# Second sublayers' soft MoE tokens: transposed by VectorE in 32-squares and placed through DRAM instead of by TensorE

## The chip, the cores and the metric

The kernel runs on one core of a Trainium2 chip. A core has five engines with a queue each: TensorE (PE; its weight loads are shown apart as PEld), VectorE (DVE), ScalarE (ACT), GpSimd (POOL) and SyncE (SP), which here issues every DMA. Engines wait for one another through semaphores, and each queue is in order. The metric is device time in microseconds (us), the median of several runs; one further execution was recorded by the hardware profiler.

## The reference

Input `x` has 8 batches of 256 tokens of 128 channels, all in float32. Six residual sublayers follow one another; the change is in the third, which computes the same as the first, with the same weights:

```python
x = x + 0.5 * _L0_ffn_ref(_layernorm(x), ...)   # soft MoE, "first sublayer"
x = x + _L0_attn_ref(_layernorm(x), ...)        # linear attention
x = x + 0.5 * _L0_ffn_ref(_layernorm(x), ...)   # soft MoE, "second sublayer": changed
x = x + 0.5 * _L1_ffn_ref(_layernorm(x), ...)   # gated MLP with two hidden layers
x = x + _L1_attn_ref(_layernorm(x), ...)        # FAVOR+ attention
x = x + 0.5 * _L1_ffn_ref(_layernorm(x), ...)
```

The soft MoE, with E = 16 experts of S = 64 slots:

```python
x = _layernorm(x, norm_g, norm_b)
se = _layernorm(slot_embeds, slot_g, slot_b) * scale
logits = einsum('bnd,esd->bnes', x, se)
dispatch = softmax(logits, axis=1)                   # over the tokens
combine = softmax(logits.reshape(b, n, -1), axis=-1) # over all slots
slots = einsum('bnd,bnes->besd', x, dispatch)
gate = gelu(einsum('besd,edf->besf', slots, Wg) + bg)
up = einsum('besd,edf->besf', slots, Wu) + bu
eout = einsum('besf,efo->beso', gate * up, Wd) + bd
out = einsum('bns,bso->bno', combine, eout)
```

## The kernel before

**Stages.** The eight batches form two groups of four. For each group `group(g)` goes through the sublayers: MoE (`layer` 0), linear attention, MoE again (`layer` 1), gated MLP (`glu`), FAVOR+ attention (`favor`), gated MLP. The two groups are interleaved, so that matmuls of one cover the dependent chains of the other.

**The MoE of one batch.** `dispatch` normalizes the 2 x 128 tokens of a batch (TT = 2 tiles `y` of 128 tokens by 128 channels): VectorE's statistics, GpSimd's inverse root (`root`), and two applications on GpSimd or VectorE. `transposed` then makes `yt`, channels by tokens, since a matmul contracts over the partitions: two TensorE transposes ("flips", L452, a matmul with the identity) into PSUM, and one `affinely` step that reads PSUM, multiplies by `norm_g`, adds `norm_b` and writes `yt` in SBUF, on ScalarE (L557) or VectorE (L559). `replicated` sends `y` through DRAM into another layout for a later matmul. Four logits steps (L670, four matmul instructions each) read `yt`. The softmax over the tokens follows (maximum on VectorE, exponentials on ScalarE, L709, division on GpSimd, 32-square transposes on VectorE), then `gather` (L749) forms the slots. `experts` fetches each expert's weights `we` (L864), runs the hidden matmuls (L878) and the down matmuls (L909), and `back.place` (L922) puts results into the slots by DMA. `combine` (L952) brings them back to tokens and adds them to `x`. In `linear`, L1000 is the last projection, whose sum `x` is what the second MoE's normalization reads.

**Transposing without TensorE.** `linear`, `glu` and `favor` already transpose their tokens in another way, `squares_turned`: VectorE transposes every 32x32 square in place (L513), one DMA spills the tile to DRAM (L516), and four DMAs place the squares into a tile of channels by tokens (L522, each 32 partitions). Both are steps on SyncE, and the placement waits for the spill's landing.

**The order.** The program first lists its steps (2490), each with its reads, its writes and an estimated cost. `ORDER` is a list of step numbers written out: a step runs on the first engine that it allows, or, where the number is negative (-1 - n), on the second. `Plan.place` goes through the list, gives each step a start by the estimates, and gives tiles their buffers from pools of fixed size (`kinds`; `k1` has 14 of 256 floats a partition, `ps` is the eight PSUM banks); `issue` emits the steps by these starts. So `ORDER` settles each engine's queue and which engine takes a movable step. Where the plan expects TensorE to wait over 700 ns for a step, `idle` (L1503) issues matmuls of the identity that compute nothing, besides 14 of them at the head.

Of the kernel before, what the change touches and what calls it, by code (L numbers as in the profile page):

```python
# [10 lines left out]
AF = mybir.ActivationFunctionType  # L11
ALU = mybir.AluOpType
AX = mybir.AxisListType
P = 128

ORDER = (
    10, 0, 3, 2, 1, 37, 38, 6, 7, 5, 9, 8, 19, 20, 12, 13, 11, 40, 39, 41, 22, 31, -22, 23, 24,
    42, 43, 62, 63, 130, 14, 16, 131, 25, 15, 17, 18, 4, 132, 133, 134, 26, 135, 44, -29, -28, 60,
    32, -34, 83, -35, 61, 138, 139, 84, -87, 1347, 161, 29, 30, 68, 1268, 140, 141, 54, 35, -86,
    89, 90, -37, 1297, 162, 69, 146, 70, 64, 65, 66, 67, -164, 73, 142, 143, 144, 145, 87, 88, 93,  # L20
    95, 114, 71, 91, -165, 167, 165, 1269, -1272, 74, 75, 76, 94, 97, 96, 166, 175, 151, 92, 98,
    147, 136, 72, 1348, -1350, -1351, 152, 173, 77, 99, 100, 192, 104, 174, 78, 82, 176, 81,
    -1271, 1272, 1273, 105, 169, 1298, -1300, -1301, 1301, 80, 101, 79, 102, 115, 106, 137, 170,
    1274, 153, 1303, 1302, 168, 103, 1353, 182, 1354, 107, 108, 154, 1276, 171, 1278, 172, 53, 45,
    1281, 1275, 1282, 1277, 1280, 1279, 1305, 1306, 148, 183, 177, 1284, 1285, 178, 1283, 1307,
    184, 155, 109, 1304, 111, 47, 112, 113, 149, 150, 156, 179, 185, 186, 180, 46, 110, 1286,
    1309, 1308, 157, 181, 187, 193, -190, 1310, 1312, 330, 1313, 320, 158, 159, 160, 190, 1292,
    191, 188, 331, 351, 334, 335, 1315, 1314, 1311, 324, 325, 194, 1331, 1332, 332, 321, 322,
    1333, 355, 362, 333, 257, 366, 215, 367, 352, 336, 57, 353, 368, 195, 354, 356, 357, 363, 364,
    348, 349, 369, 196, 1293, 219, 216, 217, 1334, 326, 341, 323, 370, 365, 246, 197, 198, 199,  # L30
    371, 1287, 1316, 372, 373, 220, 221, 299, 1351, 1352, 1317, 337, 261, 116, 262, 218, 117, 258,
    259, 345, 346, 342, 361, 338, 204, 260, 263, 232, 288, 200, 347, 247, 343, 344, 1357, 1358,
    248, 1355, 249, 350, 250, 251, 1376, 1288, 374, 233, 1377, -1379, 1294, 252, -1380, 118, 274,
    275, 1335, 358, 359, 303, 264, -1357, 1366, 1321, 304, 305, 300, 202, 277, 265, 289, 301, 302,
    1295, 292, 208, 319, 309, 290, 1336, 212, 1322, 209, 316, 119, 1363, 1318, 1359, 317, 291,
    206, 293, 1296, 1289, 1380, -1382, 236, 237, 240, 1319, 294, 1323, 210, 1290, 211, 213, 214,
    1360, 1382, 235, 313, 314, 55, 1320, 278, 306, 307, 310, 315, 120, 311, 1337, 222, 282, 318,
    312, 279, 241, 242, 1364, 327, -1362, 1291, 283, 284, 225, 229, 280, 281, 1324, 121, 230, 124,
    122, 328, 1325, 267, 226, 256, 238, 239, 234, 271, 231, 227, 228, 268, 269, 298, 1362, 272,
    1365, 339, 308, 207, 340, 253, 295, 270, 360, 254, 243, 273, 244, 203, 123, 285, 296, 125,  # L40
    286, 1371, 1372, 223, 201, 1373, 1374, 1375, 276, 1367, 266, 1326, 1327, 205, 255, -1329,
    1389, 1390, 1392, 1393, 375, 126, 127, 1384, -1331, 1368, 1400, 50, 128, 1338, 1385, 1386,
    -1388, 1395, 56, 1401, 1402, 1369, 1370, 287, 1396, 224, 129, 1397, 329, 245, 297, 377, 454,
    1388, 1391, 1403, 1329, 1404, 1398, 1399, 376, 378, 455, 402, 456, 457, 458, -460, -461, 464,
    1383, 461, 462, 379, 380, 1394, 1405, 1408, 1409, -1407, 1517, 403, 404, 428, 429, 1407, 463,
    1475, 1518, 1519, 465, 1343, 430, 405, 1521, 1411, 467, 466, -471, -382, 471, 1522, 1520,
    1523, -383, 383, 1479, 1480, 1476, 1477, 1478, 406, 1534, 1535, 1485, 1486, 1489, 1490, 1580,
    1410, 1412, 1581, -408, -409, 409, 1582, 1481, 431, 1491, 1487, 1496, 1497, 1500, 1501, 432,
    1583, -434, 1498, 468, 412, 1499, 1506, 384, 1502, 1507, 1488, 1492, 1493, 1510, 1511, 1413,
    410, 52, 1584, 1513, 1514, 1569, 1345, 1585, 1508, 1509, 1570, 1571, 1573, 1414, 1572, 411,  # L50
    414, 1537, 1464, 1503, -435, 435, 385, 1512, 1468, 469, 1465, 1504, 388, 1466, 1467, 1586,
    387, 1574, 1575, 1469, 1470, 413, 418, 1590, 436, 415, 1415, 1591, 472, 1433, -393, 1437,
    1341, 393, 1346, 1426, 1430, 51, 437, 389, 1587, 473, 440, 445, 416, 417, 1588, 1482, 419,
    390, 391, 1559, 1416, 394, 395, 1431, 1432, 1427, 396, 397, 1560, 1592, 474, 475, 398, 399,
    1483, 386, 1428, 1429, 1524, 1525, 439, 441, 1505, 1417, 1420, 1434, 1438, 1440, 1441, 1435,
    400, 1561, 1562, 1424, 1527, 1528, 420, 1454, 1436, 442, 1531, 1484, 401, 1439, 1529, 480,
    481, 421, 443, 48, 438, 483, 1548, 49, -445, 1593, 1526, 1532, 1533, 1563, 476, 477, 1515,
    1530, 1458, 1459, 1460, 482, 478, 479, 1549, 1550, 446, 447, 1552, 484, 588, 422, 589, -486,
    1553, -592, -591, 1494, 1551, 1564, 1589, 1545, 1546, 448, 449, 1443, 1565, 1455, 1456, 1342,
    1442, 1536, 490, 423, 1538, 1554, 450, -452, 1457, -492, 496, 497, 424, 425, 488, -490, 492,  # L60
    594, 1453, 1344, 452, 1339, 1340, 1450, 1451, 499, 1418, 426, 427, 453, 500, 1452, 1447, 592,
    559, 560, -562, -563, 509, 510, 1542, 501, 493, 593, 1576, 1577, 1578, -495, 1543, 504, 1539,
    1540, 596, 597, 495, 1566, 1567, 1544, 1444, 1445, 1541, 58, 598, 498, 599, 512, 604, 1547,
    1446, -512, 1448, 1579, 600, 1449, 563, 1568, -565, 601, 1419, 603, 502, 1422, 505, 513, 514,
    1555, 1471, 1472, 1473, 1556, 1425, 1474, 607, 1461, 1462, 506, 569, 1516, 1557, 567, 605,
    570, -603, 612, 568, 571, 1558, 575, 576, 1463, 572, 574, 503, 608, 609, 573, 486, 522, 523,
    1495, 606, 565, 583, 578, 507, 517, 613, 525, 515, 614, 516, 1421, 610, 543, 1621, 611, 526,
    533, 615, 616, 1620, 579, 580, 1622, 1623, 519, 520, 581, 1423, 518, 521, 1624, -1627, -1626,
    584, 566, 1647, 1646, 1648, 585, 582, 528, 1672, 1673, 534, 586, 535, 536, 1627, 587, 577,
    1594, 529, 1595, 524, 508, 527, 530, 531, 1674, 1596, 1597, 1598, 595, -1601, 617, 619, 487,  # L70
    620, 532, 1628, 1629, 537, 538, 542, -1600, 1601, 1602, 1604, 541, 1632, -619, 1675, 1676,
    -1679, -1678, 1649, 781, 1603, 1606, 621, 1679, 1680, 1650, 1651, 1610, 1605, 544, 545, -540,
    1631, -541, 666, 1652, 1656, 1653, 546, 1607, 1633, 1608, 1609, 1634, 782, 783, 1635, 785,
    -1637, 786, 787, 1611, 1612, 623, 670, 1613, 1637, 792, 796, 793, 805, 797, 798, 547, 1654,
    1630, 622, 708, 709, 710, 712, 713, 548, 624, 714, 1614, 1615, 1681, 711, 667, 668, 784, 655,
    656, 794, 1684, 659, 795, 1683, 799, 1616, 669, 1688, 1655, 1689, 1685, 686, 671, 672, 549,
    657, 658, 660, 625, 1658, 800, 661, -1663, 802, 803, 1657, 1686, 683, 1638, 1682, 1639, 1617,
    1618, 638, 1687, 550, 1619, 639, 553, 554, 725, 1659, 1660, 760, 761, 557, 726, 642, 643, 626,
    627, 684, 673, 1661, 1698, 644, 771, 1663, 1664, 739, 640, 764, 765, 1640, 1641, 645, 641,
    555, 1699, -1702, 772, 773, 674, 1665, 1690, 1691, 743, 740, 1692, 766, 762, -1701, 763, 1666,  # L80
    649, 741, 742, 1642, 1643, 1693, 1702, 1694, -1704, 804, 775, 628, 551, 744, 745, 1706, 1667,
    776, 777, 1644, 1645, 1732, 1695, 1696, 1668, 1669, 687, 629, 1708, 774, 1714, 1733, -1736,
    1697, 1816, 1817, 685, -1819, 646, -1735, 788, 789, 1738, 1819, 778, 779, 780, 675, 647, 1670,
    1671, 1707, 1704, 1710, 648, 665, 1709, 688, 689, 729, 650, 634, 1820, -1822, 632, 651, 1711,
    1712, 690, 1736, 1782, 1783, -1786, 1737, 1717, 691, 1713, 1824, 1716, -1826, 662, 663, 652,
    653, 1715, 1829, 636, 1722, 692, 693, 556, 1718, 790, 1740, 1832, 1833, 1826, 1827, 1830,
    1828, 1719, 1835, 1741, 718, -1785, 1745, 801, 1748, 1749, 1766, 1840, 635, 630, 697, 1786,
    1742, -1744, 1836, 704, 705, 1831, 1834, 1744, 1747, 1750, 654, 1767, 676, 1837, 757, 758,
# [1499 lines left out]
```

## Time and profile before

| What | Value |
|---|---|
| median of 3 runs | 716.48 us (716.41 to 716.98) |
| the profiled execution | 715.34 us |
| its span, first to last instruction | 713.6 us |
| granted TensorE clock | 1.00 |
| flips (L452) | 80: 8 for the keys, 32 in `dispatch`, 16 in `linear`, 24 in `favor` |
| flip duration, min/median/max | 272/273/333 ns |
| stand-in matmuls (L1503) | 66, from 1.6 to 45.2 us |
| 128x256 square transpose (L513), min/median | 414/446 ns |
| spill issue (L516), min/median; placement issue (L522), min/median | 325/328 ns; 557/613 ns |
| one placement, issue to landing, min/median/max | 2.1/2.8/5.3 us |
| DMA packets | 122453, of which 76048 under 512 B |

The profiled execution's time stands 1.7 us over its span, and 1.14 us under the median of the runs. Matmuls are pipelined: a flip's duration overlaps its neighbours', so what one costs TensorE is read from the start of one instruction to the start of the next. A row of the timeline gives the start, the length, the engine, the line, the operation, the tile written and those read, and, in brackets, how long the engine was idle before it and for whom. L452, L557 and the like are line numbers of the kernel before.

### The profile page before, as it was taken

To read this page: it belongs to the slowest core of one execution; us is meant where nothing else is said; L and a number is where in the kernel's file an instruction comes from. 1 tells how busy PE (TensorE), PEld (TensorE's weight loads), DVE (VectorE), ACT (ScalarE), POOL (GpSimd) and SP (SyncE) were. 2 spreads that over 40 slices of the span, in tenths; PEclk is the share of its full clock that TensorE was granted. 3 is DMA by queue.
4 is the path that set the end of the run, shared out by engine and by line. 5 is a ranking of instruction groups with operands and counts; after the bars stand their busy time and mean duration, and the time that the engine had idled before them with its cause. 6 is when DMAs were issued, how large, how long until landed. Compare 5 with 4: busy or idle time off the path is not lost.

```text
span 713.6 us, 14278 instructions
## 1 busy us (share of the span) xinstructions
PE 705.1 (99%) x5218; PEld 606.1 (85%) x5218; DVE 492.5 (69%) x1075; ACT 398.1 (56%) x775; POOL 331.9 (47%) x443
## 2 busy tenths in 40 slices
PE   8999999999999999999999999999999999999998
PEld 6889899998999998998889799786787878869787
DVE  6998867668998779983625444895777777865342
ACT  4978975364892638974536563365243653443421
POOL 6750947345665357465765103535444253342210
PEclk9999999999999999999999999999999999999999
DMA  4464752567263646557354121233213142151000
GB/s 131 135 194 150 210 143 56 184 183 201 65 162 90 175 128 171 126 127 232 110 184 108 45 60 23 45 82 78 65 38 75 26 113 47 38 120 44 8 1 30
DMA packets 122453, 75.00 MB, mean 105 GB/s; under 512 B 76048, under 2 KB 110224, under 8 KB 122384
## 3 DMA queue, kind: packets, MB, share of 16 engines
q1 hardware_dynamic: 122384, 74.09, 39.1%
q8 instruction: 41, 0.67, 0.4%
q14 instruction: 28, 0.23, 0.1%
HBM read 54.06 MB, written 11.62 MB: 92 GB/s over the span
## 4 chain that ended last, share of the span: by engine, by line
PE 89%; ACT 3%; DVE 3%; DMA 2%; POOL 1%; issue 1%; SPq 1%; DVEq 0%; ACTq 0%; POOLq 0%
PE ps L1167 27%; PE ps L878 14%; PE ps L952 8%; PE ps L909 7%; PE ps L749 7%; PE ps L670 5%; PE ps L1265 4%; PE ps L1237 4%; PE ps L1240 4%; ACT comb L709 2%; DMA we<-in_We 1%; PE ps L1342 1%; PE ps L1392 1%; PE ps L452 1%; PE ps L1427 1%; PE ps L1000 1%
## 5 line engine op out<-in xcount | busy, mean ns | idle before, releaser
L878 PE MATMUL ps<-slots,we 128*128 128x256 f32 x512 | 121.1, 380 | 0.8 <-DVE k L915 0.4
L878 PEld LDWEIGHTS ps<-slots,we 128*128 128x128 f32 x512 | 93.4, 190 | 13.3 <-issue 1.0
L1167 PE MATMUL ps<-comb,slots 128*128 128x256 f32 x448 | 103.4, 381 | 0.0
L1167 PE MATMUL ps<-comb,comb 128*128 128x256 f32 x448 | 103.1, 379 | 0.0
L1167 PEld LDWEIGHTS ps<-comb,slots 128*128 128x128 f32 x448 | 83.2, 190 | 13.4 <-issue 2.8
L1167 PEld LDWEIGHTS ps<-comb,comb 128*128 128x128 f32 x448 | 83.8, 190 | 12.6 <-issue 1.7
L884 ACT ACTIVATE k<-ps,small 128x256 f32<-128x256 f32 x128 | 55.8, 475 | 61.5 <-PE ps L878 52.8
L837 POOL TENSOR_TENSOR comb<-comb,k 128x1024 f32<-128x1024 f32 x32 | 75.2, 2362 | 19.1 <-DMA k<-m 8.8
L889 DVE SCALAR_TENSOR_TENSOR k<-ps,small,k 128x256 f32<-128x256 f32 x128 | 57.2, 475 | 31.2 <-ACT k L884 30.4
L722 POOL TENSOR_TENSOR comb<-comb,sm 128x1024 f32<-128x1024 f32 x32 | 60.3, 1897 | 35.7 <-DVE sm L717 28.5
L1181 DVE TENSOR_TENSOR comb<-ps,k 128x512 f32<-128x512 f32 x48 | 32.7, 686 | 56.2 <-PE ps L1167 36.7
L909 PEld LDWEIGHTS ps<-we,k 128*128 128x128 f32 x512 | 64.1, 192 | 2.9 <-issue 0.7
L709 ACT ACTIVATE comb<-comb,sm 128x256 f32<-128x256 f32 x128 | 63.5, 506 | 3.1 <-DVE sm L701 2.5
L909 PE MATMUL ps<-we,k 128*128 128x128 f32 x512 | 64.9, 275 | 0.0
L670 PE MATMUL ps<-k,seT 128*128 128x256 f32 x256 | 61.0, 382 | 1.1 <-ACT k L557 0.9
L457 ACT COPY k<-ps 128x512 f32<-128x512 f32 (+2 forms) x45 | 23.0, 517 | 67.7 <-PE ps L1167 49.2
L952 PEld LDWEIGHTS ps<-slots,comb 128*128 128x128 f32 x512 | 58.7, 192 | 1.5 <-issue 0.7
L952 PE MATMUL ps<-slots,comb 128*128 128x129 f32 x512 | 59.4, 276 | 0.1
L749 PE MATMUL ps<-comb,k 32*128 32x256 f32 x1024 | 58.9, 378 | 0.0
L749 PEld LDWEIGHTS ps<-comb,k 32*128 32x128 f32 x1024 | 53.2, 185 | 3.6 <-ACT slots L557 0.4
L670 PEld LDWEIGHTS ps<-k,seT 128*128 128x128 f32 x256 | 46.8, 190 | 8.6 <-ACT k L557 2.2
L1189 ACT ACTIVATE comb<-comb 128x512 f32<-128x512 f32 x48 | 29.2, 627 | 38.7 <-DVE comb L1181 38.5
(148 smaller groups left out, 1246.3 us busy)
## 6 DMA issues: line engine op xcount, KB each, us to landing
we<-in_We SPq DMA_DIRECT2D x64, 448.0 KB, 4.1
k<-y SPq DMA_DIRECT2D x64, 128.0 KB, 2.9
slots<-k SPq DMA_DIRECT2D x128, 64.0 KB, 2.4
t<-comb SPq DMA_DIRECT2D x8, 512.0 KB, 2.9
k<-t SPq DMA_DIRECT2D x32, 128.0 KB, 3.2
y<-k SPq DMA_DIRECT2D x16, 128.0 KB, 2.5
k<-m SPq DMA_DIRECT2D x8, 256.0 KB, 4.0
t<-k SPq DMA_DIRECT2D x16, 128.0 KB, 1.7
```

The lines of the kernel that those rows point to most:

```text
L670: mm(pl.ap[:, j, :], seT[:, 2 * u + j].rearrange("p k s -> p (k s)"), yt.ap, start=True, stop=True,)
L709: nc.scalar.activation(ex.ap[:, 4 * h + j, :], comb.ap[:, 4 * h + j, :], AF.Exp, bias=mx.ap[:, j : j + 1], accum_out=mx.ap[:, 4 + j : 5 + j],)
L722: return nc.gpsimd.tensor_tensor(ex.ap[:, part], ex.ap[:, part], mx.ap[:, 8:12].unsqueeze(2).to_broadcast([P, 4, N]), ALU.mult,)
L749: mm(po.ap[:, k], yr.ap[rows, TT * (c % 4) + c // 4, :], ex.ap[rows, :, 32 * c : 32 * c + 32], start=(c == 0), stop=(c == N // 32 - 1), ti ...
L837: return nc.gpsimd.tensor_tensor(raw, raw, mb.ap[:, k].unsqueeze(1).to_broadcast([P, 4, N]), ALU.subtract)
L878: mm(pe.ap[:, m, :], we.ap[:, ts(2 * m + c, P)], sl.ap[:, j, k, :, 0:S], start=True, stop=True,)
L884: nc.scalar.activation(ga.ap, pe.ap[:, 0, :], AF.Gelu, bias=bg[:, e, c : c + 1])
L889: nc.vector.scalar_tensor_tensor(ht.ap[:, c, :], pe.ap[:, 1, :], bu[:, e, c : c + 1], ga.ap, ALU.add, ALU.mult,)
L909: mm(po.ap[:, r, :], ht.ap[:, c, ts(r, P)], we.ap[:, ts(4 + c, P)], start=(c == 0), stop=(c == 1),)
L952: mm(po.ap[:, t, 0 : D + 1], comb.ap[:, j, ts(t, P)], eo()[:, j, q, 0 : D + 1], start=(j == 0), stop=(j == NJ - 1),)
L1167: mm(bank.ap[:, o], w(k)[:, c, ts(o, P)], rhs().rearrange("p (c n) -> p c n", c=2)[:, c, :], start=(start and o + c == 0), stop=(stop and ...
L1181: nc.vector.tensor_tensor(C(i, k)(), bank.ap.rearrange("p o n -> p (o n)"), other(), ALU.add)
```

## The change

The `dispatch` of the second sublayer (`plan.tag[1] == 1`, eight batches) takes the way of `squares_turned`. VectorE transposes the squares from `y` into `yt`, out of place, since `replicated` still reads `y`; `yt` is spilled, and the placements write back into the same `yt`; the affine step then runs in place in SBUF. `port=True` tells the plan that, on VectorE, that step keeps GpSimd's next step behind it. A second sublayer's batch has two steps more than before, 2506 in all; `ORDER` is another list throughout, and `k1` has 16 buffers. The first sublayers' `dispatch` keeps the flips.

```diff
 ORDER = (
-    10, 0, 3, 2, 1, 37, 38, 6, 7, 5, 9, 8, 19, 20, 12, 13, 11, 40, 39, 41, 22, 31, -22, 23, 24,
...
+    11, 10, 1, 13, 0, 14, 37, 2, 38, 12, 5, 25, 26, 3, 19, 40, 39, 41, 15, 42, 16, 17, 18, 60, 7,
...
-        "k1": (256, 14),
+        "k1": (256, 16),
...
-    def squares_turned(z, n, cells, dst, out):
+    def squares_turned(z, n, cells, dst, out, src=None):
...
-        step({"DVE": 58 + 1.07 * n}, lambda _: nc.vector.transpose(z(), z()), cells, cells)
+        if src:
+            step({"DVE": 58 + 1.07 * n}, lambda _: nc.vector.transpose(z(), src[0]()), src[1], cells)
+        else:
+            step({"DVE": 58 + 1.07 * n}, lambda _: nc.vector.transpose(z(), z()), cells, cells)
...
     def transposed(y, n, affine=False, squares=False):
         yt = Buf("k1" if n == TT else "k2", (P, n * P))
+        if squares and affine:
+            squares_turned(
+                lambda: yt.ap, n * P, [yt], lambda: yt.ap, [yt],
+                (lambda: y.ap[:, 0:n].rearrange("p t d -> p (t d)"), [(y, t) for t in range(n)]),
+            )
+            affinely(lambda: yt.ap, lambda: yt.ap, [yt], [yt], n * P, True)
+            return yt
...
-    def affinely(dst, src, r, w, n):
+    def affinely(dst, src, r, w, n, port=False):
         def run(e):
             if e == "ACT":
-                nc.scalar.activation(dst(), src(), AF.Identity, bias=nb, scale=ng)
-            else:
-                nc.vector.tensor_scalar(dst(), src(), ng, nb, ALU.mult, ALU.add)
-
-        step({"ACT": act(n, True) + 87, "DVE": dve(n, 120)}, run, [*r, "ng"], w)
+                return nc.scalar.activation(dst(), src(), AF.Identity, bias=nb, scale=ng)
+            return nc.vector.tensor_scalar(dst(), src(), ng, nb, ALU.mult, ALU.add)
+
+        step({"ACT": act(n, True) + 87, "DVE": dve(n, 120)}, run, [*r, "ng"], w, port=port)
...
-        yt = transposed(y, TT, True)
+        yt = transposed(y, TT, True, plan.tag[1] == 1)
```

By the two lists, TensorE's queue before the first expert matmul holds 24 logits steps, six flip pairs of `dispatch` and four gathers in the old order, and 26, seven and four in the new. Steps that may run on two engines are split differently: of the evacuations of PSUM 114 run on ScalarE and 38 on VectorE in the old list, 104 and 48 in the new; of the applications of the normalization 74 on GpSimd and 30 on VectorE, then 63 and 41.

## The prediction

> **What bounds the kernel.** I read the page's busy shares and its chain of waits first, then the stretches of the span, then TensorE's instructions in order of time.
>
> ```profile
> PE 705.1 (99%) x5218; PEld 606.1 (85%) x5218; DVE 492.5 (69%) x1075; ACT 398.1 (56%) x775; POOL 331.9 (47%) x443
> ...
> PE 89%; ACT 3%; DVE 3%; DMA 2%; POOL 1%; issue 1%; SPq 1%; DVEq 0%; ACTq 0%; POOLq 0%
> ```
>
> TensorE (PE) is busy for 705.1 of 713.6 us, and 89% of the chain that ends last is PE. The stretches say the same piece by piece; the columns are the stretch, its length, and busy time with instruction counts for PE, PEld, DVE, ACT and POOL:
>
> ```profile
> 10.00:50.00 40.00, 39.13 (x348) 32.48 (x350) 38.90 (x59) 34.91 (x103) 29.26 (x45) 1.00 0.48 135
> ...
> 150.00:192.00 42.00, 41.76 (x269) 38.23 (x269) 34.95 (x98) 27.36 (x49) 17.62 (x31) 1.00 0.61 161
> ...
> 240.00:285.00 45.00, 44.62 (x285) 41.04 (x284) 36.48 (x94) 27.98 (x64) 26.98 (x32) 1.00 0.53 147
> ...
> 330.00:460.00 130.00, 130.00 (x743) 110.34 (x743) 62.96 (x162) 62.83 (x91) 57.65 (x76) 1.00 0.35 96
> ```
>
> The granted clock is 1.00 throughout. So the time is what TensorE executes plus the few places where it waits. Those places lie early: between 10 and 50 us it runs stand-in matmuls (L1503) that compute nothing, put where the plan expects it to wait.
>
> ```profile
> 14.83 0.61 PE L1503 MATMUL ps<-ident 128*128 128x128 f32 x4
> 15.46 0.76 PE L452 MATMUL ps<-ident,k 128*128 128x128 f32 x2
> ...
> 19.77 0.83 PE L1503 MATMUL ps<-ident 128*128 128x128 f32 x6
> 20.86 2.86 PE L670 MATMUL ps<-k,seT 128*128 128x256 f32 x12 [0.26 <-ACT k L557]
> ...
> 32.40 1.16 PE L1503 MATMUL ps<-ident 128*128 128x128 f32 x8
> 33.78 6.67 PE L670 MATMUL ps<-k,seT 128*128 128x256 f32 x28 [0.23 <-ACT k L557]
> ...
> 44.31 1.16 PE L1503 MATMUL ps<-ident 128*128 128x128 f32 x8
> 45.39 7.19 PE L749 MATMUL ps<-comb,k 32*128 32x256 f32 x128
> ```
>
> From each stand-in to the next real matmul: 0.63, 1.09, 1.38 and 1.08 us, and 0.76 for one more at 26.42; 4.94 us in all.
>
> **Removed from TensorE: 16 flips.** The second-layer `dispatch` runs for eight batches, with TT = 2 flips each. The price of one comes from start to start:
>
> ```profile
> 244.36 1.05 PE L909 MATMUL ps<-we,k 128*128 128x128 f32 x8
> 245.25 0.38 PE L452 MATMUL ps<-ident,k 128*128 128x128 f32 x2
> 245.47 0.61 PE L1029 MATMUL ps<-WqkvT,k 128*128 128x128 f32 x4
> ```
>
> Two flips push the next matmul back by 245.47 - 245.25 = 0.22 us, so 8 x 0.22 = 1.76 us leave the bound engine. This is the safest term: in the two stretches that hold them, 150 to 192 and 240 to 285, TensorE is idle for only 0.24 and 0.38 us. If something else filled the place, the gain would be 0; that is a rival below. The Trainium skill, "TensorE: Matmul & The Clock Gate", Part 4 (PE-mode transpose), gives about 275 ns for one transpose in a kernel; the trace has 272/273/333 ns for these as durations but 0.11 us from start to start, so an estimate by the page (16 x 0.275 = 4.4 us) would count the overlap with their neighbours as gain, and I do not use it.
>
> **Added off TensorE.** Per batch: one 128x256 square transpose on VectorE, one spill to DRAM, four placements of 32 KB, and the affine step as before but reading SBUF. The same parts exist today in `linear` and `favor`: the transpose takes 0.446 us (median), so VectorE gets 8 x 0.446 = 3.6 us against 492.5 busy of 713.6. SyncE issues take 0.33 for the spill and about 0.61 for each placement, 0.33 + 4 x 0.61 = 2.8 us a batch, 22 us in all. From 150 to 190 SyncE's own issues already sum to about 25 of 40 us, so four batches (11 us) fit, but not loosely. The affine step keeps its count. All this costs nothing as long as the tokens land before their logits stand at the head of TensorE's queue.
>
> **The cover.** Old way, flip to affine to logits: about 1 us. New way, by rows: in the first five undisturbed cases of today's squares the time from transpose start to the last landing was 6.8 to 8.2 us, for example here (SyncE, start and length; the transpose began at 124.39, the last piece landed at 132.40):
>
> ```profile
> 124.86 0.34 SPq L516 DMA_DIRECT2D t<-k  x1
> 125.24 0.43 SPq L864 DMA_DIRECT2D we<-in_We  x1
> 126.66 2.61 SPq L522 DMA_DIRECT2D k<-t  x4
> ```
>
> Before it come the batch's last projection (0.61), its add (0.41), the statistics on VectorE (0.94), GpSimd's root (0.19 + 0.19 + 0.70) and two applies (0.90); after it the affine step (0.55). That is 4.5 us around the transfer, 11.3 to 12.7 in all. The new order leaves this much TensorE work between a batch's last projection and its first logits, counted step by step from the listed order and priced by start-to-start rows (0.864 us for a logits or hidden step, 0.45 for a down step): 14.7, 12.8, 17.9 and 18.5 us for batches 0 to 3, and 14.9, 12.0, 22.3 and 11.3 for 4 to 7. So batch 7 could be late by up to 12.7 - 11.3 = 1.4 us and batch 5 by 0.7; at the short end nobody is. I take 0.3 us, from the short end, since the 32 placements that the kernel has today made TensorE wait only once, for 0.5 us (L1298). Bounds: 0 to 2.1. [...]
>
> **What waits behind the wait.** SyncE's queue is in order. In the new order one to four other steps stand between each spill and its own placement: expert weights (L864), token copies (L638) and, for batches 0, 1, 2 and 6, an expert's `back.place` (L922), which waits for VectorE. The spill itself waits for the transpose, and weight fetches stand behind it. Today SyncE waits 109.1 us in total at L516 for such transposes and TensorE waits 0.2 us for weights, so this cover is large.
>
> **The order.** Modes of TensorE's array change 50 times in the old list and 49 times in the new: no term. Before the first expert matmul the old list has 24 logits steps and 6 flip pairs, the new one 26 and 7. That is 2 x 0.864 + 0.22 = 1.95 us of work moved ahead of a point that falls at 54.3 us and is reached with 4.94 us of stand-ins. If the point stays, 1.95 us is gained. Against it: ScalarE also gets one softmax half, a key step, an affine step and an evacuation more before that point, 1.97 + 0.56 + 0.57 + 0.59 = 3.7 us, and from 25 to 43 it runs without a gap. It does wait 2.51 and 1.57 us for the gathers at 46 to 53, so 4.08 us could take it. The gain has bounds of +4.94 (all stand-ins vanish) and -3.7 (ScalarE pushes the point back by all of it); I take half of 1.95, 1.0 us. VectorE's and GpSimd's changes elsewhere have no price of their own: a gain is bounded by TensorE's idle time between 50 and 660 us, 1.5 by the stretches, a loss by the slower rival below, and I take 0. The two more `k1` tiles cost SBUF alone.
>
> **Sum.** -1.76 + 0.3 - 1.0 = -2.46. The profiled execution took 715.34 us (span 713.6 and 1.7 around it), which becomes 712.9. The median of the runs is 1.14 above the profiled one; so 716.48 - 2.46 = 714.0.
>
> **Rivals.**
> - *Flips only.* The head of the kernel stays where ScalarE puts it: 716.48 - 1.76 + 0.3 = 715.0. For it: ScalarE's gapless stretch. Against it: its 4.08 us of waiting at the end of that stretch.
> - *No gain.* The flips' 1.76 us turn into short waits of the same size, as the tokens now come from a chain several times as long: 716.5. For it: SyncE's many issues from 150 to 190. Against it: today's single 0.5 us wait.
> - *Slower: a placement is caught in SyncE's queue.* At 137.33 and 227.48 us a transpose began whose placement landed 14.0 and 11.5 us later, since other steps stood between. If the longer happens to batch 5, 14.0 + 4.5 - 12.0 = 6.5 us of stall fall on TensorE: 716.48 - 1.76 + 6.5 = 721.2. It decides from a stall of 1.76 + 1.43 = 3.2 us (0.2% is 1.43). For it: `back.place` between spill and placement. Against it: batch 6, with the most between, has 22.3 us of cover.
>
> **How the numbers follow.** A measurement of this kernel can tell about 0.2% from no change: faster is below 715.05, slower above 717.91. The forecast has 0.52, flips only 0.20, no gain 0.14, caught placement 0.14. The forecast's own range is 712.3 to 715.2. Faster: 0.50 of the forecast and 0.12 of flips only, 0.62; same: 0.02 + 0.08 + 0.14 = 0.24; slower 0.14. The range goes down to 711.4 (a further 2.6 us, when most of the stand-ins go) and up to 717.0, which takes in no gain and a small stall and leaves out nearly all of the caught placement.
>
> **What would show it.** TensorE's `ps<-ident,k` group falls from 80 to 64; the logits (L670, some lines further down) wait for `k<-t` or the affine step for under half a microsecond in total; stand-ins before the first expert matmul shrink below 4.94 us with that matmul still near 54.3. I am wrong if TensorE's idle time at the logits grows past 2 us, if the first expert matmul comes later than 55.3, or if weights (`we<-in_We`) start to hold TensorE.

## The result, and the profile after

| | before | after |
|---|---|---|
| median of seven runs | 716.48 us (715.90 to 717.54) | 719.04 us (717.64 to 720.03) |
| the profiled execution, its span | 715.34, 713.6 us | 719.04, 717.3 us |

The ratio is 1.0032, with a 95% interval of 1.0021 to 1.0044: the change makes the kernel slower by a third of a per cent. The forecast was 714.0 with a range of 711.4 to 717.0, so both the sign and the range missed.

The page's busy times and its chain of waits, after:

```profile
PE 705.7 (98%) x5200; PEld 605.5 (84%) x5200; DVE 499.3 (70%) x1093; ACT 407.2 (57%) x780; POOL 330.0 (46%) x435
...
PE 53%; DMA 3%; DVE 2%; ACT 1%; SPq 1%; issue 1%; POOL 0%; DVEq 0%; POOLq 0%
```

TensorE issues 18 matmuls fewer (16 flips and two stand-ins), and yet the span is 3.7 us longer. The 53% of the chain can't be held against the 89% before: the profile follows the chain after only back to 281.73 us, and its shares sum to 61%. The stretches of the kernel after (stretch, length, busy time and count for PE, PEld, DVE, ACT and POOL, granted clock, DMA share, GB/s) say where TensorE now stands still:

```profile
10.00:50.00 40.00, 38.02 (x328) 32.12 (x328) 37.79 (x60) 35.27 (x105) 28.34 (x43) 1.00 0.47 133
115.00:150.00 35.00, 34.06 (x319) 31.38 (x318) 23.46 (x67) 16.51 (x29) 19.02 (x27) 1.00 0.46 140
150.00:192.00 42.00, 41.69 (x260) 37.73 (x259) 33.64 (x97) 29.39 (x51) 17.91 (x25) 1.00 0.65 174
240.00:285.00 45.00, 44.68 (x281) 41.05 (x280) 38.82 (x106) 28.29 (x61) 24.45 (x31) 1.00 0.56 154
285.00:335.00 50.00, 47.89 (x483) 43.28 (x482) 36.56 (x78) 32.88 (x85) 28.32 (x25) 1.00 0.55 160
```

Two of the same stretches in the kernel before, which the prediction didn't show:

```profile
115.00:150.00 35.00, 35.00 (x324) 32.73 (x323) 21.90 (x61) 15.03 (x28) 19.38 (x29) 1.00 0.44 129
...
285.00:335.00 50.00, 49.93 (x494) 45.77 (x493) 37.06 (x80) 35.81 (x82) 28.91 (x26) 1.00 0.59 155
```

By busy time, the stretches that hold the changed work, 150 to 192 and 240 to 285, are as full as before. Most of what is lost lies from 115 to 150, before any second-sublayer placement is issued (the first is at 170.9 us), and from 285 to 335: 0.94 and 2.04 us of idle time more. TensorE's waits in the kernel after (line and cause: us in total, times, longest) name the missing things:

```profile
PE ps L888 <- DMA we<-in_We: 1.7, 3, 0.9
PE ps L1513 <- POOL ident masks.py:199: 1.6, 1, 1.6
PE ps L962 <- DMA slots<-k: 1.2, 1, 1.2
PE ps L680 <- ACT seT L603: 1.1, 2, 0.7
PE ps L680 <- ACT k L568: 0.9, 3, 0.4
PE ps L759 <- issue: 0.5, 1, 0.5
PE ps L759 <- DMA k<-y: 0.5, 1, 0.5
```

Before, one such row was for a transfer among these three:

```profile
PE ps L878 <- DMA we<-in_We: 0.2, 1, 0.2
```

Three transfers now hold TensorE for 3.4 us, where before it was 0.2: expert weights (`we`, L888), slot copies by `back.place` (`slots<-k`, the combine at L962) and token copies by `replicated` (`k<-y`, the gather at L759). None of the three is what the change touches. The placed tokens hold it hardly at all: of the 0.9 us at the logits (L680) for the affine step (L568), only 0.2 lies after 55 us.

For a finer sum every kind of matmul is priced by its pitch, its regular distance from start to start (0.216 us for a 128x256 one, 0.112 for a 128x128 one, 0.054 for one of a gather), and the rest of TensorE's time, from its first matmul on, is called unused; it takes in the stand-ins, short waits and slow pitches. The pitched time falls by 1.79 us, as 16 flips should. The unused time by the stretch in which a matmul starts, in us:

| | 0-55 | 55-115 | 115-150 | 150-285 | 285-335 | 335-end | sum |
|---|---|---|---|---|---|---|---|
| before | 15.97 | 0.73 | 0.35 | 1.97 | 2.00 | 10.51 | 31.5 |
| after | 15.96 | 1.06 | 1.76 | 3.09 | 5.06 | 10.06 | 37.0 |

So -1.79 + 5.46 gives the 3.67 us by which the two spans differ; 3.1 of the 5.46 are lost from 285 to 335, 1.4 from 115 to 150 and 1.1 from 150 to 285. (The medians differ by 2.56, because the profiled execution before was 1.14 under its median and the one after is at its median.)

**Where the 285 to 335 stretch loses it.** SyncE's queue in the kernel after, in order of time (start, length, line, transfer, count):

```profile
299.75 10.02 SPq L932 DMA_DIRECT2D slots<-k  x13
309.82 2.03 SPq L653 DMA_DIRECT2D k<-y  x4
311.95 0.37 SPq L809 DMA_DIRECT2D q<-sm  x1
315.51 0.30 SPq L812 DMA_DIRECT2D k<-q  x1
317.75 0.32 SPq L826 DMA_DIRECT2D m<-k  x1
319.12 0.34 SPq L829 DMA_DIRECT2D k<-m  x1
319.51 1.85 SPq L653 DMA_DIRECT2D k<-y  x4
```

and TensorE beside it:

```profile
309.05 1.16 PE L962 MATMUL ps<-slots,comb 128*128 128x129 f32 x8
311.36 6.49 PE L962 MATMUL ps<-slots,comb 128*128 128x129 f32 x56 [1.16 <-DMA slots<-k]
...
325.22 0.70 PE L759 MATMUL ps<-comb,k 32*128 32x256 f32 x4
326.38 4.26 PE L759 MATMUL ps<-comb,k 32*128 32x256 f32 x60 [0.46 <-DMA k<-y]
```

The combine at 311.36 waits for a slot copy issued in the block of 13 before. Then four tiny transfers of the softmax's maxima (L809 to L829) occupy SyncE from 311.95 to 319.46, although their issues sum to 1.33 us: each waits for the one before to land or for VectorE, and what stands behind waits too. Behind them stands a batch's token copy, issued at 319.51, and its gather, interrupted at 325.22, takes 5.36 us from its start to the next combine's, where the one at 317.78 took 3.67. The Trainium skill, "DMA: Bandwidth & Descriptors", Anatomy of one DMA — SWDGE (gpsimd) path, says that any semaphore wait happens on the issuing engine's sequencer before the transfer is dispatched. These rows, of SyncE's queue, agree: four transfers that wait keep the queue to themselves for 7.5 us.

### The profile page after: what moved, and what is told of

It is laid out like the page before. It is cut to its first block, busy times and chain, and to the rows that moved or that the text cites. A ratio compares the mean times of both kernels' runs of the same rounds, so it can differ in the third digit from the quotient of the medians.

```text
span 717.3 us, 14292 instructions
## 1 busy us (share of the span) xinstructions
PE 705.7 (98%) x5200; PEld 605.5 (84%) x5200; DVE 499.3 (70%) x1093; ACT 407.2 (57%) x780; POOL 330.0 (46%) x435
## 4 chain that ended last, share of the span: by engine, by line
PE 53%; DMA 3%; DVE 2%; ACT 1%; SPq 1%; issue 1%; POOL 0%; DVEq 0%; POOLq 0%
PE ps L1177 27%; PE ps L1275 4%; PE ps L888 4%; PE ps L1250 4%; PE ps L1247 3%; PE ps L962 3%; PE ps L919 2%; PE ps L1352 1%; DMA k<-y 1%; PE ps L1437 1%; PE ps L1402 1%; PE ps L759 1%; PE ps L1308 1%; PE ps L1010 1%; DMA q<-sm 0%
## 5 line engine op out<-in xcount | busy, mean ns | idle before, releaser
L888 PE MATMUL ps<-slots,we 128*128 128x256 f32 x512 | 120.3, 380 | 1.7 <-DMA we<-in_We 1.7
L888 PEld LDWEIGHTS ps<-slots,we 128*128 128x128 f32 x512 | 94.3, 191 | 14.8 <-DMA we<-in_We 1.3
L680 PE MATMUL ps<-k,seT 128*128 128x256 f32 x256 | 60.8, 384 | 2.1 <-ACT seT L603 1.1
L759 PE MATMUL ps<-comb,k 32*128 32x256 f32 x1024 | 60.4, 379 | 1.2 <-issue 0.5
L962 PE MATMUL ps<-slots,comb 128*128 128x129 f32 x512 | 59.7, 277 | 1.2 <-DMA slots<-k 1.2
L962 PEld LDWEIGHTS ps<-slots,comb 128*128 128x128 f32 x512 | 58.3, 192 | 3.0 <-issue 2.6
L759 PEld LDWEIGHTS ps<-comb,k 32*128 32x128 f32 x1024 | 53.7, 185 | 6.1 <-issue 2.5
L680 PEld LDWEIGHTS ps<-k,seT 128*128 128x128 f32 x256 | 46.6, 190 | 10.4 <-ACT k L568 2.0
L1162 POOL TENSOR_TENSOR comb<-comb 128x512 f32<-128x512 f32 x19 | 24.1, 1269 | 60.4 <-ACT comb L1199 21.9
```

The source lines that it names most:

```text
L680: mm(pl.ap[:, j, :], seT[:, 2 * u + j].rearrange("p k s -> p (k s)"), yt.ap, start=True, stop=True,)
L759: mm(po.ap[:, k], yr.ap[rows, TT * (c % 4) + c // 4, :], ex.ap[rows, :, 32 * c : 32 * c + 32], start=(c == 0), stop=(c == N // 32 - 1), ti ...
L888: mm(pe.ap[:, m, :], we.ap[:, ts(2 * m + c, P)], sl.ap[:, j, k, :, 0:S], start=True, stop=True,)
L962: mm(po.ap[:, t, 0 : D + 1], comb.ap[:, j, ts(t, P)], eo()[:, j, q, 0 : D + 1], start=(j == 0), stop=(j == NJ - 1),)
```

## The experiments

Each run was timed against the kernel before on its own chip (medians of before: 716.05 to 716.29 us). "Sequence" means the order of steps in an engine's queue.

**e1: the new list with the old flips.** The change undone in the computation, kept in the list. The 16 flip steps take the places of the placements (for one batch that of the square transpose).

```diff
         if squares and affine:
-            squares_turned(...)
-            affinely(lambda: yt.ap, lambda: yt.ap, [yt], [yt], n * P, True)
+            for k in range(3):
+                (flips_of if k == (0 if early else 2) else nothing)()
+            affinely(lambda: yt.ap, lambda: pt.ap.rearrange("p t c -> p (t c)"), [pt], [yt], n * P)
             return yt
```

> The changed kernel with its new order and its 16 buffers, but the second sublayers' tokens are turned by TensorE again: the flips stand where the placement stood in the list (for batch 3 where VectorE's transpose stood), and the eight transposes, spills and 32 placements are gone. Theory Q (SyncE's queue: the added spills and placements make later expert weights, slot copies and token copies start late, and TensorE waits for those): the 1.76 us of flips come back, but TensorE's waits from 240 to 335 us (about 5.4 us of time without useful matmuls there in the changed kernel, 2.4 in the kernel before) fall to the old size, so 716.5 to 718, clearly below 719.04 + 1.76 = 720.8. Rival O (the new order is bad by itself, whatever turns the tokens): nothing is relieved, 720 to 721.

Measured: 721.19 us, ratio 1.0069 (1.0054 to 1.0083), 0.2 over the range expected if the order is bad by itself, and well above what was expected if SyncE's added transfers are the cause. Without these transfers the kernel is 2.15 us slower than with them. So the squares are a gain at this list, and the list by itself costs nearly 5 us. The 2.15 are more than the price of the flips. One wait comes from the flips' place in this list: behind the flips at 193.22 TensorE stands still until ScalarE has done an affine step, here and again in e10, and neither in the kernel before nor in the changed one:

```profile
PE ps L933 <- ACT k L582: 1.5, 1, 1.5
```

TensorE again waits for weights (2.0 us), and 2.3 us go unused around a gather at 325 us.

**e3: one placement in place of four.**

```diff
         def place(_):
             squares = there.rearrange("(a i) (t f) j -> f i t a j", a=4, f=4)
+            if src:
+                nc.sync.dma_start(dst(), there.rearrange("p k j -> p (k j)"))
+                return
             for f in range(4):
```

> The changed kernel, where each second-sublayer placement is one DMA of whole rows instead of four DMAs of 128-byte pieces: the tokens then stand in the order of the spill, so the MoE's logits are of other data; all instructions and bytes else are the same. It takes three issues of about 0.6 us a batch from SyncE and most of the small packets. Theory Q: the waits from 240 to 335 us shrink, 714.5 to 717. Rival O: within 0.5 us of 719.0.

The tokens then stand in the order of the spill, so this kernel computes something else. Measured: 719.10 us, 1.0041 (1.0028 to 1.0054), no relief in the total. The single issue takes a median of 0.39 us where four take some 2.4, so eight batches free about 16 us of SyncE between 173 and 287 us, and the time doesn't move. By its profile two things cancel. From 285 to 335 us no wait of TensorE for a transfer is left (2.2 us in the changed kernel), and the unused time there falls from 5.06 to 2.85. From 55 to 285 it rises from 5.91 to 8.19: weights hold TensorE for 2.1 us before 150, ahead of anything that the edit touches (0.9 in the changed kernel), and `linear`'s own tokens for 1.0 between 150 and 192. Why that is so stays open; the part before 150 can only be a difference between executions. A side result: whole rows land in a median of 3.3 us, the 128-byte pieces of the real placement in 2.5 us each.

**e4: 32 tiny transfers more.**

```diff
         def place(_):
...
+            if src:
+                for f in range(4):
+                    nc.sync.dma_start(junk[f], ident[0:1, 0:32])
```

> The changed kernel with four more DMAs behind each second-sublayer placement, of 128 bytes each into DRAM that nothing reads: SyncE issues 32 more, about 0.33 us each, 1.3 us a batch, and next to no bytes are added. Theory Q (SyncE's issue time is what is short): slower, by 2 to 5 us. Rival B (bandwidth or small packets, not issue time): within 1 us of 719.0. Rival O: the same within 1 us.

Measured: 727.10 us, 1.0146 (1.0124 to 1.0169), 8.1 us over the changed kernel (5.1 in the profiled execution, the fastest of these runs), more than the 2 to 5 expected. The 32 issues take a median of 0.250 us and 9.5 us in sum, so most of it reaches the end. TensorE's waits for weights rise to 4.0 us and those at the logits for the affine step to 2.6; from 285 to 335 its waits for transfers are 4.4 us, against 2.2 in the changed kernel and none in e3. In the total, taking SyncE time away at these places gained nothing, and adding some cost nearly all of it. A queue behaves so when the steps behind are due at once: they can't come earlier than what they themselves wait for, and any delay in front of them passes on. That reading is argued; the numbers are measured.

**e5, e6, e7: other lists.** If the list is what costs, another list should give the gain back. For e5, steps were moved at random within their dependencies, starting from the new list, and kept where an estimate fell: the plan's own estimate of the kernel's length, half as it is and half with SyncE's issues 6% longer, transfers 3% longer and results 0.1 us later ("with margin"). e6 uses the plan's estimate as it is, from another start. e7 is the kernel before, its list searched with margin. The first numbers of the lists:

```diff
-    11, 10, 1, 13, 0, 14, 37, 2, 38, 12, 5, 25, 26, 3, 19, 40, 39, 41, 15, 42, 16, 17, 18, 60, 7,
+    1, 11, 10, 13, 14, 0, 37, 38, 5, 25, 26, 2, 12, 3, 19, 40, 39, 41, 42, 7, 130, 20, 16, 15,
...
-    11, 10, 1, 13, 0, 14, 37, 2, 38, 12, 5, 25, 26, 3, 19, 40, 39, 41, 15, 42, 16, 17, 18, 60, 7,
+    0, 37, 38, 11, 3, 19, 20, 1, 13, 39, 21, 22, 7, 130, 14, -41, 23, 2, 12, 24, 16, 15, 41,
...
-    10, 0, 3, 2, 1, 37, 38, 6, 7, 5, 9, 8, 19, 20, 12, 13, 11, 40, 39, 41, 22, 31, -22, 23, 24,
+    11, 0, 37, 3, 38, 19, 6, 31, 1, 13, 20, 39, 40, 41, 21, 22, 23, 2, 12, 42, 14, 7, 130, 24,
```

> The changed kernel with another list, and nothing else: searched on from the changed one, where a list counts by its plan's length as before and by that length with SyncE's issues 6% longer, transfers' time in the queue 3% longer and their results 0.1 us later, half each. Theory M (the changed list fits the estimates so closely that SyncE and the transfers have no time to spare, and each one that is late reaches TensorE): the squares' gain appears, 711.5 to 714.5, with TensorE's useless time from 55 to 335 us under 5 us (9.9 in the changed kernel, 4.1 in the kernel before). Rival S (the squares' own transfers are what TensorE waits for, in any list): 716.5 or more. Rival R (lists scatter by some us on the chip whatever they were scored by): anything from 714 to 720.

> As the run with margin, from another starting list (the old one carried over), the same search and as long, but scored by the plan's own estimates alone. Theory M: no better than the changed kernel by more than 2 us, 717 to 721. Rival R: as likely at 714 as at 720. Rival S: 717 to 721 too.

> The kernel before (flips, 14 buffers) with only its list searched on with the same margin. Theory M: 713 to 716, a little faster than the kernel before, and slower than the squares with margin by the flips' 1.76 us, give or take 1. Rival S: faster than the squares with margin.

Measured: e5 714.69 us (0.9981, 0.9969 to 0.9993), e6 720.10 (1.0054, 1.0042 to 1.0065), e7 719.14 (1.0039, 1.0027 to 1.0051). e5 is faster than the kernel before, though 0.2 above what was expected, and its unused time from 55 to 335 us, 8.3 us, lies between the changed kernel's 11.0 and the 5.1 before. e6 is in its range, but the rival that lists scatter by some us allows both numbers. e7 is a miss: the same estimate made the kernel before slower by 2.8 us. In e7 TensorE waits 1.2 us for weights and 1.1 for issue at the hidden matmuls near 130 us, and 1.4 for the slot embeddings at the head. So a list moved on all engines can lose as much as it gains, whatever the estimate says. These three run against one another in everything at once, so the next run moved one queue alone.

**e8: SyncE's sequence alone.** From the changed kernel, only SyncE's steps were moved, by the estimate with margin; 182 of 305 keep their sequence. TensorE, VectorE, ScalarE and GpSimd execute the same instructions in the same sequence as in the changed kernel.

```diff
-    11, 10, 1, 13, 0, 14, 37, 2, 38, 12, 5, 25, 26, 3, 19, 40, 39, 41, 15, 42, 16, 17, 18, 60, 7,
+    1, 11, 10, 0, 13, 14, 37, 38, 2, 12, 5, 25, 26, 3, 19, 9, 40, 39, 41, 15, 42, 16, 17, 18,
```

> The changed kernel, where only SyncE's queue stands in another sequence (the same search with margin, moving SyncE's steps alone); TensorE, VectorE, ScalarE and GpSimd have their instructions in the same sequence as the changed kernel. Theory M, if SyncE's sequence is most of it: 715 to 717.5. If the other queues' sequences have no margin either, 717.5 to 719. Rival S and rival R: 718 to 720.

Measured: 713.84 us (712.49 to 714.69), 0.9969 (0.9957 to 0.9980), better than expected. One queue's sequence takes 5.2 us off the changed kernel, its loss of 2.56 and as much again (5.0 by the differences from the kernel before on each run's own chip). SyncE in e8 at the place shown above, and TensorE there:

```profile
305.26 0.35 SPq L813 DMA_DIRECT2D q<-sm  x1
305.65 4.40 SPq L657 DMA_DIRECT2D k<-y  x8
310.09 0.43 SPq L816 DMA_DIRECT2D k<-q  x1
313.75 0.32 SPq L830 DMA_DIRECT2D m<-k  x1
315.68 0.34 SPq L833 DMA_DIRECT2D k<-m  x1
```

```profile
305.58 7.41 PE L966 MATMUL ps<-slots,comb 128*128 128x129 f32 x64
312.93 3.74 PE L763 MATMUL ps<-comb,k 32*128 32x256 f32 x64
316.59 3.84 PE L966 MATMUL ps<-slots,comb 128*128 128x129 f32 x32
320.36 3.74 PE L763 MATMUL ps<-comb,k 32*128 32x256 f32 x64
324.03 3.84 PE L966 MATMUL ps<-slots,comb 128*128 128x129 f32 x32
```

All eight token copies now go out while the first maximum is on its way, done at 310.05 instead of 321.36, and combine and gather follow one another without a gap. Of TensorE's waits for transfers none is left among the largest:

```profile
PE ps L1517 <- POOL ident masks.py:199: 1.6, 1, 1.6
PE ps L684 <- ACT seT L607: 1.0, 2, 0.6
PE ps L1035 <- ACT k L1056: 0.7, 1, 0.7
PE ps L684 <- ACT k L572: 0.5, 2, 0.3
```

**e13: the same search again, another seed.** A single such list could be a lucky one, so it was drawn once more.

```diff
-    11, 10, 1, 13, 0, 14, 37, 2, 38, 12, 5, 25, 26, 3, 19, 40, 39, 41, 15, 42, 16, 17, 18, 60, 7,
+    1, 11, 10, 13, 14, 0, 37, 38, 2, 12, 5, 25, 3, 26, 19, 40, 39, 41, 15, 42, 16, 17, 18, 60,
```

> The changed kernel again with SyncE's sequence alone searched anew from the changed kernel's own, by the same score (half the estimate itself, half the estimate with SyncE's issues 6% longer, transfers 3% longer and results 0.1 us later), from another seed. It shares 183 of 305 steps in sequence with the changed kernel's and 186 with the first such run's. The estimate is 708.29 us for all three lists; with the longer issues it is 715.0 us for the changed kernel's, 711.05 for both searched ones. My theory, that the 5 us are slack in SyncE's queue, which this score sees: 713.8 us again (712.5 to 715.5). Rival, that such lists scatter by a few us for reasons that the score does not see, and the first was a lucky draw: 715.5 to 720, nearer to 719.0 than to 713.8 in half the cases.

Measured: 713.20 us (711.91 to 714.49), 0.9961 (0.9947 to 0.9976). It repeats. This is the fastest version of the study.

**e10: the flips at e8's SyncE sequence.** The edit is e1's, with e8's list; it completes a table of two by two.

> The list of steps of the run that differs from the changed kernel in SyncE's sequence alone, with the 16 turns back on TensorE (VectorE's squares, their spill and placements do nothing). If what TensorE saves by the turns is its own 16 flips of 0.11 us and nothing else, this run takes 713.84 + 1.76 = 715.6 us (714.7 to 716.5). Rival, the squares' DMAs and waits cost something even in the new SyncE order: 715.0 or less, so that the turns are worth under 1 us. Rival, the new SyncE order only helps with the squares: 719 to 721, as with the changed kernel's own list.

Measured: 716.01 us, 0.9994 (0.9985 to 1.0003).

| | changed kernel's list | e8's list |
|---|---|---|
| flips on TensorE | 721.19 | 716.01 |
| squares on VectorE | 719.04 | 713.84 |

The squares gain 2.15 and 2.17 us; SyncE's sequence costs 5.18 and 5.20. The four were timed on different chips; by the differences from the kernel before on each chip the squares gain 2.37 and 2.23, and SyncE's sequence costs 5.15 and 5.01. So the two effects add within the noise, which is some 1 us a run; that the medians add to within 0.02 is luck. In e10 the wait of e1 is there again:

```profile
PE ps L937 <- ACT k L586: 1.5, 1, 1.5
```

By the profiles, e10 leaves 1.1 us more unused than e8 from 150 to 192, where this wait begins, and 1.0 less from 192 to 285. The squares' 2.2 us are thus the flips' 1.79 and several waits that nearly cancel. And e10 is as fast as the kernel before: with this SyncE sequence the rest of the new list is neither better nor worse than the old list. Whether the old list too would gain from a searched SyncE sequence was not run.

**e11 and e12: which part of the sequence.** e8's SyncE sequence up to a gather at about 225 us and the changed kernel's own afterwards (e11), and the reverse (e12).

SyncE's sequence in words (the edit itself is in the numbers of `ORDER`):

```
changed kernel:  [changed kernel, up to step 542] [changed kernel, from step 542]
e11:             [e8, up to step 542]             [changed kernel, from step 542]
e12:             [changed kernel, up to step 542] [e8, from step 542]
```

> The changed kernel with SyncE's new sequence up to the gather of the first second-sublayer batch of layer 0 (about 225 us), and from there on in the changed kernel's own sequence as far as the steps are the same. All other engines' sequences stay. My theory: slack is missing at several places, so this part gives back what TensorE lost to expert weights at 134 us, at 168 and 193 us and in the head (2.5 to 3.3 us), and not what it loses at 284 to 330 us: 716.0 us (715.2 to 717). Rival, one place alone: 719 if all the loss is in the backlog at 285 to 330 us, 714 if it all follows from the late weights at 134 us.

> The mirror of it: the changed kernel's own SyncE sequence up to the same gather at about 225 us, and the new one from there. My theory: the weights at 134 us stay late, and the slot and token copies at 306 to 326 us come in time, which gives 2.5 to 3.3 us: 716.0 us (715.2 to 717). Rival, one place alone: 714 if all the loss is in the backlog at 285 to 330 us, 719 if it all follows from the late weights at 134 us.

Measured: e11 716.96 us (1.0013, 1.0003 to 1.0024), e12 717.69 (1.0023, 1.0011 to 1.0035). The early part gives back 2.1 us and the late part 1.4, less than expected: e11 is at the upper end of the 715.2 to 717 us, e12 above it. Neither part is the one place. The unused time by stretch, in us, as above:

| | 0-55 | 55-115 | 115-150 | 150-285 | 285-335 | 335-end | sum |
|---|---|---|---|---|---|---|---|
| e11, early | 16.75 | 0.74 | 0.34 | 2.73 | 2.87 | 10.07 | 33.5 |
| e12, late | 15.74 | 1.46 | 2.30 | 3.68 | 1.86 | 10.61 | 35.6 |
| e8, both | 15.34 | 0.73 | 0.35 | 2.80 | 1.14 | 10.09 | 30.5 |
| e13 | 15.24 | 0.73 | 0.35 | 2.14 | 1.33 | 10.11 | 29.9 |

In e12 the stretch from 115 to 150 stays bad, as it must. In e11 the late stretch falls from 5.06 to 2.87 us although SyncE's sequence there is that of the changed kernel; that the queue comes to it earlier is a likely reason, and not shown. The two gains sum to 3.5 of 5.2 us; what the rest is, beyond their being needed together, stays open. (The profiled executions of e8, e11 and e13 are 1.3 to 1.4 us under their medians and that of e12 is at its median, so three of the rows flatter their kernels.)

**e9: the squares in the old list.** The changed code, with the list of the kernel before, in which the new steps are put in (16 of them, a spill and a placement for each of eight batches; the expectation's 32 is a slip) and the logits shifted by a few places.

```diff
-    11, 10, 1, 13, 0, 14, 37, 2, 38, 12, 5, 25, 26, 3, 19, 40, 39, 41, 15, 42, 16, 17, 18, 60, 7,
+    10, 0, 3, 2, 1, 37, 38, 6, 7, 5, 9, 8, 19, 20, 12, 13, 11, 40, 39, 41, 22, 31, -22, 23, 24,
```

> The changed kernel's code with the list of the kernel before, in which only the 32 new steps (spill and placement, 16 times) were put in and the 32 logits steps shifted by a few places to make room. By the turns alone it would be 716.5 - 1.8 = 714.7 us. The path from turned squares to logits is longer (spill about 2 us, placement about 2.5 us and their waits in SyncE's queue) and nothing else was shifted to cover it, so my theory expects TensorE to wait at the second sublayers' logits: 720 to 726 us, with waits at the logits of several us in sum.

Measured in one execution: 732.58 us, worse than expected. SyncE, then TensorE, at the worst place:

```profile
279.47 0.38 SPq L525 DMA_DIRECT2D t<-k  x1
279.94 2.94 SPq L937 DMA_DIRECT2D slots<-k  x2
283.36 2.57 SPq L531 DMA_DIRECT2D k<-t  x4
```

```profile
282.94 3.73 PE L1518 MATMUL ps<-ident 128*128 128x128 f32 x32
288.30 1.99 PE L685 MATMUL ps<-k,seT 128*128 128x256 f32 x8 [1.62 <-DVE k L574]
```

A batch's tokens are spilled at 279.47, two slot copies stand before their placement, and TensorE runs 32 stand-ins and then waits: 288.30 - 282.94 = 5.4 us without use. It is the largest piece of the 19 us that TensorE leaves unused here beyond the kernel before. This is the slower rival of the prediction as it was worded, a placement caught in SyncE's queue. With the old list as carried over here the change loses; the list that it came with avoids this wait and pays elsewhere.

## Why the prediction was wrong

- **Sixteen flips, -1.76: right.** `ps<-ident,k` falls from 80 to 64 and the pitched time by 1.79 us. The start-to-start price was the right one; the duration of a flip, 0.273 us, would have given 16 x 0.273 = 4.4. The two pairs of runs give 2.15 and 2.17 us, which other waits go into as well. The squares on VectorE took 0.445 us each (0.446 expected).
- **Late tokens, +0.3: right.** 0.2 us of waits after 55 us. The placements landed in a median of 2.5 us, against 3.3 us for whole rows in e3. The Trainium skill ("VectorE: DVE Perf Modes", The three transpose paths) calls a plain strided copy 19 times slower than the DMA transpose when the innermost stride of the destination is large; these placements write 128 bytes in a row, so no run here shows that case. One price in the cover was wrong, on the safe side: a down step is eight matmuls, by the row at 244.36 us 245.25 - 244.36 = 0.89 us and not 0.45. With four and three down steps in their covers, batches 5 and 7 had about 13.8 and 12.6 us instead of 12.0 and 11.3, so hardly any batch could be late.
- **The head, -1.0: wrong, it is about 0.** 1.95 us of logits and flips were moved ahead of the first expert matmul, and that matmul moved by as much, past the 55.3 us set as a mark. TensorE before, then after:

```profile
52.51 1.99 PE L670 MATMUL ps<-k,seT 128*128 128x256 f32 x8
54.34 3.83 PE L878 MATMUL ps<-slots,we 128*128 128x256 f32 x17
```

```profile
53.58 2.86 PE L680 MATMUL ps<-k,seT 128*128 128x256 f32 x12
56.28 1.89 PE L888 MATMUL ps<-slots,we 128*128 128x256 f32 x8
```

  56.28 - 54.34 = 1.94 us. In the eight other profiles with this TensorE sequence in the head (e1, e3, e4, e8, e10 to e13) the first expert matmul starts between 55.56 and 57.07 us, so the head is 0 within 0.8 us, and the close match is luck. "Flips only" had this right. TensorE's unused time before 55 us is 16.0 us in both. That ScalarE holds the head, as that rival said, fits its 35.27 busy us from 10 to 50 (34.91 before), but no run separated it.
- **The order, "I take 0": the step that failed.** By e1 the new list with the old flips costs 4.7 us against the kernel before (721.19 - 716.48), and 4.71 - 2.15 is the 2.56 that was measured. By e8 and e10 this lies in SyncE's sequence: against one searched for the same code it costs 5.2 us, with the squares and with the flips. Two readings led to the 0. The bound by TensorE's idle time was used for gains only; a loss was to come from the changed steps alone, although the list was another throughout. And "SyncE waits 109.1 us in total at L516 and TensorE waits 0.2 us for weights, so this cover is large" took waiting time for spare time. In this queue, waiting at the head is blocking: the token copies behind the four waiting transfers went out 7.5 us after the first of these, and in e8, where they went out ahead of the waits, they held nobody up. In e8 SyncE waits 114.0 us at that line, in the changed kernel 123.4, so the sum says next to nothing. What a queue can spare is seen from each transfer's landing to the matmul that needs it, and that was not looked at for weights, slot copies and token copies.
- **The slower rival** named the right queue and the wrong victim: the placements came in time, the other transfers didn't. The mark "weights start to hold TensorE" showed it, at 1.7 us.

That e8 and e13 land within a microsecond of the 714.0 doesn't make the forecast's sum right: they have the flips' gain at 2.2 and the head's at 0.

## What to carry to other kernels

When a change comes with a new order of everything, price the order before the edit: for each transfer, compare its landing with the start of what needs it, and look for transfers that stand behind one that waits. A queue's total waiting time is not its slack. And where a measured loss has no cause in the edited steps, run the new order with the old computation: that one run parts the two.

## What the runs showed of the hardware

- Tiny transfers weren't free in this queue: 32 of 128 bytes, 9.5 us of issues in sum, cost 8.1 us in the median.
- The wait for the first inputs differs between executions. In e8 and e11 SyncE issues the same transfers in the same sequence up to the first flips. From the first stand-ins at 1.6 us to these flips, with 40 stand-ins in between, it took 5.95 us in e8's profile and 7.48 in e11's. A profile's span can so be off by 1.5 us before the first useful matmul, which is why the comparisons here rest on medians and on the stretches after 55 us.
